# A four-layer graph network on one core: layer 3's rows for the first 20 node tiles stay in SBUF for layer 4

## The chip, the core and the metric

The kernel runs on one core of a Trainium2 chip. Its engines run in parallel, each through its own instructions in their order: PE (TensorE, matrix products into PSUM), ACT (ScalarE), DVE (VectorE), POOL (GpSimd, here the issuer of the gathers) and SP (SyncE, here an issuer of DMAs; ACT issues DMAs too). The metric is the device time of one execution in microseconds, the median of several runs. A profiled execution gives the lines that are quoted below.

## The reference

The input is x, 6250 nodes of 256 features, and 100,000 edges (src, dst) that are sorted by dst. Low-numbered nodes have by far the most edges. What is computed:

```python
h = relu(layernorm(x))
h = h @ W1_self + mean(h[src] by dst) @ W1_neigh + b1                    # layer 1
hp = relu(h @ W2_pool + b2_pool)
h = h @ W2_self + max(hp[src] by dst) @ W2_neigh + b2                    # layer 2, max-pooling
h = ((sum(h[src] by dst) + h) / (deg + 1)) @ W3_neigh + b3               # layer 3
h = h @ W4_self + mean(h[src] by dst) @ W4_neigh + b4                    # layer 4
out = x + h @ W_fc + b_fc
```

All of it is in fp32, with hidden width 512.

## The kernel before

The nodes are cut into 49 tiles of 128. The weight matrices that follow each other without a nonlinearity are multiplied with each other first, so that layers 3 and 4 have only sums over edges left to do on the nodes.

A sum over edges is done in one of two ways. For the first tiles, which have most edges (20 tiles in layer 3, `H3`; 22 in layer 4, `H4`), it is dense: a matrix A of edge counts, built before in fp8 and kept in DRAM as `tab_a`, is multiplied with the rows of all 49 source tiles (`dense`, the matmuls of L566 and L574 into `pd`). For the other tiles, POOL gathers the source rows, 128 edges at a time (L492), and PE adds them up with a one-hot matrix (L510 and L513 into `pg`); after every four gathers DVE adds the sum to `acc` (L542 and L544). `sums` writes both into one program: per gather one matmul of the gathered rows, and between them an even share of the dense matmuls, which a `Hub` hands out.

Layer 3 leaves, for each of the 49 tiles, 128 rows of two halves (`halves`: a rounded value and what the rounding left), 512 fp32 numbers, 256 KB a tile. `done3` writes them to DRAM as `tab_s`. For the 20 dense tiles it first adds `acc3`, 20 tiles of SBUF of the same size that hold the part of the sum that was made during the max-pooling layer.

Layer 4 (the block under `with tc.tile_pool(name="fl4"`) needs all 49 tiles of rows twice: the gathers read single rows from `tab_s`, and the dense matmuls need each tile whole in SBUF, as `Z4[s]`. Ten tiles (33 to 42) never leave SBUF: `done3` writes them into `zt33` and `zt38`. The other 39 are read back from `tab_s` by six loads on SP's queue (`resident`, L1817; `zt<-tab_s` in the profile). A is read in strips: `ac` is one strip, for one result tile and 5 to 7 source tiles, loaded through ACT's queue (L1785) nine strips ahead, and ACT widens it to `af` (L1794) four strips ahead. There are ten `ac` and six `af` buffers, so a strip can be widened when PE has finished the strip six before it.

The order of the source tiles is `order`: first the ten kept ones, then the loaded ones, for result tiles 0 to 3 together (their four sums lie in four PSUM banks), then tile after tile. The kept tiles' matmuls for result tiles 0 to 3, 40 of them, stand ahead of the first gathered matmul; the other 1038 are shared out over the gathers, four to five for each of the 266. The ring of gathered rows has 14 places: POOL's gather number n waits until PE has used number n-14.

When a result tile is complete, `done4` loads its rows of x and of `xq` (`xr` and `q`, through ACT's queue), DVE adds all up (L1910 and L1912), and SP stores it (L1915).

One rule of the built program matters here. Each DMA that SP or ACT issues takes one of eight semaphores in turn, in the program's order, and one that takes a semaphore waits until the semaphore's last user has landed. These semaphores are called counters below; rows of the order name them DMAHW0 to DMAHW7. So a load of a strip on ACT's queue can wait for a `zt` load on SP's, although it uses nothing of it, and whatever stands behind it on ACT waits too.

Of the kernel before, what the change touches and what calls it, by code (L numbers as in the profile page):

```python
# [9 lines left out]
F32 = mybir.dt.float32  # L10
# [3 lines left out]
F32R = mybir.dt.float32r  # L14
# [7 lines left out]
P = 128  # L22
# [15 lines left out]
def _edges_below(n, E, N):  # L38

    f = math.sqrt(min(n, N) / N)  # L40
    return E * f, Z_SIGMA * math.sqrt(E * f * (1.0 - f))
# [37 lines left out]
def fast_path(  # L79
# [18 lines left out]
    FH = W1_self.shape[1]  # L98
    FO = W_fc.shape[1]
    NT = (N + P - 1) // P  # L100
# [15 lines left out]
    for d in range(NT):  # L116
        m, s = _edges_below(d * P, E, N)
        m1, s1 = _edges_below((d + 1) * P, E, N)
# [9 lines left out]
    for d in range(NT):  # L128
        m, s = _edges_below(d * P, E, N)
        m1, s1 = _edges_below((d + 1) * P, E, N)  # L130
# [7 lines left out]
    H1, H3, H4 = HUB  # L138
# [524 lines left out]
    with ExitStack() as pro:  # L663
# [195 lines left out]
        nk = max(RB1, RB * P - RB1)  # L859
# [239 lines left out]
    with ExitStack() as on:  # L1099
# [35 lines left out]
        def done1(d, acc):  # L1135
# [37 lines left out]
            with behind(ended):  # L1173
                for k in range(KI):
# [11 lines left out]
                        lambda acc, d=d: todo.append(done1(d, acc)), extra=3)  # L1186
# [4 lines left out]
        hub = Hub(made.rest() + work)  # L1191
# [100 lines left out]
    span4 = ctx.enter_context(tc.tile_pool(name="span4", bufs=1))  # L1292
    upto3 = ctx.enter_context(ExitStack())
    span3 = upto3.enter_context(tc.tile_pool(name="span3", bufs=1))
# [2 lines left out]
    nc.scalar.dma_start(srcE, stash_e[0, :, jb - JC * P : T - JC * P].bitcast(I32))  # L1297
    keyE = span4.tile([P, T - jb], F32, name="keyE")
    nc.scalar.dma_start(keyE, stash_e[1, :, jb - JC * P : T - JC * P])
    acc3 = [span3.tile([P, FH], F32, name=f"acc3_{d}") for d in range(H3)]  # L1300
    begun = set()

    def add3(d, v):
# [12 lines left out]
    with tc.tile_pool(name="fl2c", bufs=1) as ck, ExitStack() as late:  # L1316
# [350 lines left out]
        hub = Hub(first, 12)  # L1667
# [12 lines left out]
        for b in reversed(range(NB)):  # L1680
# [3 lines left out]
            for s0 in range(0, tb, G2):  # L1684
                X = (xmore if at // G2 % 2 else xpool).tile([P, G2, FH], F32, name="X2")
                for k in range(G2):
# [27 lines left out]
                    if at == MADE_AT:  # L1714
                        for _ in steps:
# [3 lines left out]
                                                    name="kept_rows", bufs=1))  # L1719
# [101 lines left out]
    with ExitStack() as on:  # L1821
        psd = on.enter_context(tc.tile_pool(name="psd3", bufs=2, space=PSUM))
        psg = on.enter_context(tc.tile_pool(name="psg3", bufs=3, space=PSUM))
        psm = on.enter_context(tc.tile_pool(name="psm3", bufs=2, space=PSUM))
        one_tag[id(psm)] = "pm"
        zk = on.enter_context(tc.tile_pool(name="fz4", bufs=1, side="right"))
        Z4 = {}
        z4_kept = ((33, 38), (38, 43))
        z4_late = ((0, 7), (7, 14), (14, 20), (20, 27), (27, 33), (43, NT))
        for s0, s1 in z4_kept:  # L1830
            zt = zk.tile([P, s1 - s0, 2 * FO], F32R, name=f"zt{s0}", bufs=1)
            Z4.update({s: zt[:, s - s0, :] for s in range(s0, s1)})

        with tc.tile_pool(name="fl3", bufs=2) as wk:
            def done3(d, acc):
                q = wk.tile([P, FH], F32, name="q", bufs=2)
                if d < H3:
                    nc.vector.tensor_add(q, acc, acc3[d])
                    nc.vector.scalar_tensor_tensor(q, q, rgcn[:, d : d + 1], qrow,
                                                   op0=ALU.mult, op1=ALU.add)  # L1840
                else:
                    if d in Z3:
                        z = Z3[d]
                    else:
                        z = wk.tile([P, 3 * FH], BF16, name="zown", bufs=1)
                        with tc.issue_after(kept_stores[-1].ins):
                            nc.sync.dma_start(z, tab_r[d * P : (d + 1) * P, :])
                        yield 1
                        yield 1
                        yield 1  # L1850
                    if d < NT - 4:
                        for part in range(3):
                            nc.vector.tensor_add(acc, acc, z[:, part * FH : (part + 1) * FH])
                            yield 1
                    else:
                        own = bank(psm, "pm", "pm_own")
                        for part in range(3):
                            nc.tensor.matmul(own, ident_b, z[:, part * FH : (part + 1) * FH],
                                             start=(part == 0), stop=(part == 2))
                        yield 1  # L1860
                        nc.vector.tensor_add(acc, acc, own)
                    nc.vector.scalar_tensor_tensor(q, acc, rgcn[:, d : d + 1], qrow,
                                                   op0=ALU.mult, op1=ALU.add)
                q2 = Z4[d] if d in Z4 else wk.tile([P, 2 * FO], F32R, name="q2")
                halves(q[:, FO:], FO, q2)
                nc.sync.dma_start(tab_s[d * P : (d + 1) * P, :], q2.bitcast(F32))
                nc.sync.dma_start(xq[d * P : (d + 1) * P, :], q[:, :FO])
                yield 1

            late = ((0, 4), (4, KEPT), (EARLY[1], 45), (45, NT))  # L1870
            Z3 = {s: kept_rows[0][:, s, :] for s in range(KEPT)}
            with tc.issue_after(kept_stores[-1].ins):
                for s0, s1 in ((EARLY[1], NT),):
                    Z3.update(resident(wk, tab_r, FH, s0, s1))
            block = stream(wk, [(d, s0, s1) for d in range(H3) for s0, s1 in late], wk,
                           lambda s: s < KEPT)
            todo = []
            work = []
            for d in range(H3):
                work += dense([s for s0, s1 in late for s in range(s0, s1)], lambda s, d=d: block(d, s), lambda s: Z3[s], FH, psd,  # L1880
                              lambda acc, d=d: todo.append(done3(d, acc)), own=d,
                              halved=range(KEPT))
            sums(wk, psg, tab_r, FH, srcE, keyE, jb, H3, done3, 11, Hub(work), wait=14, todo=todo,
                 rest=12)

        upto3.close()
        settle(zk, on.enter_context(tc.tile_pool(name="flp", bufs=1, space=PSUM)))
        with tc.tile_pool(name="fl4", bufs=2) as wk:
            loaded4 = {}

            def load4(d):
                n = P if d < NFULL else NREM
                xr = wk.tile([P, FI], F32, name="xr4", bufs=10)
                nc.scalar.dma_start(xr[:n, :], x[d * P : d * P + n, :])
                q = wk.tile([P, FO], F32, name="q4", bufs=10)
                nc.scalar.dma_start(q[:n, :], xq[d * P : d * P + n, :])
                loaded4[d] = n, xr, q

            def done4(d, acc):
                for i in range(d, min(d + 3, H4 if d < H4 else NT)):  # L1900
                    if i not in loaded4:
                        load4(i)
                return finish4(d, acc)

            def finish4(d, acc):
                n, xr, q = loaded4.pop(d)
                yield 1
                yield 1
                yield 1
                nc.vector.tensor_add(xr[:n, :], xr[:n, :], q[:n, :])  # L1910
                for c in range(0, acc.shape[1], FO):
                    nc.vector.scalar_tensor_tensor(xr[:n, :], acc[:n, c : c + FO],  # L1912
                                                   rmean[:n, d : d + 1], xr[:n, :],
                                                   op0=ALU.mult, op1=ALU.add)
                nc.sync.dma_start(out[d * P : d * P + n, :], xr[:n, :])  # L1915

            order = [*z4_kept, *z4_late]
            first = range(4)
            block = stream(zk, [(d, *c) for c in order for d in first]
                           + [(d, *c) for d in range(4, H4) for c in order],  # L1920
                           wk, deep=9, ahead=4)
            todo = []
            parts4 = []
            for d in range(H4):
                parts4.append(dense([s for s0, s1 in order for s in range(s0, s1)],
                                    lambda s, d=d: block(d, s), lambda s: Z4[s], FO, (psd, psm)[d // 2 % 2],
                                    lambda acc, d=d: todo.append(done4(d, acc)), wide=True))
            nk = sum(s1 - s0 for s0, s1 in z4_kept)
            cuts = [sum(s1 - s0 for s0, s1 in order[:i]) for i in range(len(order) + 1)]
            hub = Hub([w for a, b in zip(cuts, cuts[1:]) for d in first for w in parts4[d][a:b]]  # L1930
                      + [w for p in parts4[4:] for w in p])
            hub.advance(4 * nk)
            for s0, s1 in z4_late:
                Z4.update(resident(wk, tab_s, FO, s0, s1))
            sums(wk, psg, tab_s, FO, srcE, keyE, jb, H4, done4, 14, hub, wait=4, todo=todo,
                 rest=8, wide=True)
# [643 lines left out]
```

## Time and profile before

| What | Value |
|---|---|
| runs before | 2724.58 us median of 3 (2719.38 to 2725.16) |
| the profiled execution's own time | 2732.06 us |
| its span | 2730.3 us |
| busy share of the span | PE 84%, DVE 76%, POOL 68%, ACT 48% |
| granted TensorE clock, mean | 0.924 of full |
| first gather of layer 4 | 2360.83 us from the start |
| last gather of layer 4 | 2712.28 us |
| bytes moved by DMA | 809.90 MB |

A row of a timeline reads: start in us, duration in us, engine, line of the kernel, operation, what it writes and reads, how many were merged into the row; in brackets, how long the engine had been idle and what ended that. A name such as SPq or ACTq is the engine's queue of DMAs. In a table of waits the engine and line stand on the left, what it waited for on the right, then the sum in us, the number of waits and the longest.

### The profile page before, as it was taken

The page shows a single profiled execution, that of the slowest core. Times are in us where ns is not written, and L with a number is a line of the kernel's source. Part 1 is how long each engine was busy: PE and PEld are TensorE (multiplying, and loading weights), DVE is VectorE, ACT ScalarE, POOL GpSimd, SP SyncE. Part 2 cuts the span into 40 slices and gives each one's busy share as a digit, 9 for nine tenths or more (in the row PEclk, how much of TensorE's full clock was granted, in tenths as well). Part 3 has the DMA queues.
Part 4 walks back from the last instruction along what each step waited for, and adds up shares of the span by engine and source line. Part 5 has one row for each costly group of instructions (what it writes and reads, how often), then busy time and mean ns, then how long its engine had stood idle before and what let it go on. Part 6 is the DMA issues. An engine that isn't in the chain of part 4 may idle for free.

```text
span 2730.3 us, 37722 instructions
## 1 busy us (share of the span) xinstructions
PE 2303.3 (84%) x10402; PEld 1436.1 (53%) x10402; DVE 2084.6 (76%) x5540; ACT 1301.6 (48%) x2859; POOL 1858.7 (68%) x2169
## 2 busy tenths in 40 slices
PE   4688999999787366566978999898799999879987
PEld 2356666777443132222645666655345445568766
DVE  8888777776489898888678998888467777557666
ACT  4467777764278888696422333232211111234443
POOL 5477777777567677677656676566477777667775
PEclk8799999999898578778989999999899999989999
DMA  8567777777699899899989999999799999999996
GB/s 272 157 178 206 209 206 212 217 222 232 200 356 341 295 343 346 290 322 358 342 288 305 339 343 318 283 321 311 283 380 385 378 383 363 333 364 351 315 302 216
DMA packets 365625, 809.90 MB, mean 297 GB/s; under 512 B 56238, under 2 KB 154646, under 8 KB 365372
## 3 DMA queue, kind: packets, MB, share of 16 engines
q0 software_dynamic: 143248, 501.86, 56.3%
q1 hardware_dynamic: 145928, 215.57, 21.7%
q10 hardware_dynamic: 76228, 89.96, 9.7%
q8 instruction: 85, 1.39, 0.2%
q14 instruction: 136, 1.11, 0.1%
HBM read 602.51 MB, written 205.46 MB: 296 GB/s over the span
## 4 chain that ended last, share of the span: by engine, by line
PE 49%; DMA 26%; DVE 13%; issue 5%; ACT 2%; POOL 2%; ACTq 0%; DVEq 0%; POOLq 0%; SPq 0%
PE pd L574 18%; PE pg L513 11%; DMA X<-rows,srcIf 9%; DMA ring<-tab_h,srcT 4%; DVE run L1669 3%; PE pm_hp L1175 3%; PE pm_prf L1558 3%; DMA rows<-X 2%; DMA xr<-in_x 2%; PE pm_hp L1169 2%; PE pb L349 2%; DVE acc L544 2%; DVE X L1669 2%; DMA out<-xr 2%; PE pm_prf L1552 2%
## 5 line engine op out<-in xcount | busy, mean ns | idle before, releaser
L1688 POOL DMA_INDIRECT X<-rows,srcIf x782 | 744.5, 952 | 368.0 <-issue 143.8
L1669 DVE SCALAR_TENSOR_TENSOR run<-run,samef,X 128x512 f32<-128x512 f32 x758 | 573.1, 756 | 52.8 <-DMA X<-rows,srcIf 47.1
L492 POOL DMA_INDIRECT ring<-tab_h,srcT x474 | 456.7, 963 | 150.1 <-issue 53.2
L513 PE MATMUL pg<-ring,hot 128*128 128x259 bf16 (+1 forms) x2292 | 475.1, 316 | 45.9 <-DMA ring<-tab_h,srcT 34.8
L544 DVE SCALAR_TENSOR_TENSOR acc<-pg,M,acc 128x256 f32<-128x256 f32 (+2 forms) x617 | 314.6, 536 | 79.5 <-PE pg L513 71.1
L492 POOL DMA_INDIRECT ring<-tab_r,srcE x290 | 292.1, 1007 | 117.1 <-issue 51.8
L1794 ACT CAST af<-ac 128x768 fp32r<-128x768 fp8e4 (+3 forms) x216 | 172.7, 805 | 384.7 <-DMA ac<-tab_a 193.4
L513 PEld LDWEIGHTS <-hot 128*128 128x128 bf16 x2292 | 214.0, 98 | 231.6 <-issue 108.7
L492 POOL DMA_INDIRECT ring<-tab_s,srcE x266 | 255.4, 960 | 110.5 <-PE pg L510 34.8
L566 PE MATMUL pd<-zt,af 128*128 128x512 f32 x1078 | 300.7, 402 | 33.5 <-ACT af L1794 30.5
L1669 DVE SCALAR_TENSOR_TENSOR X<-X,samef,run 128x512 f32<-128x512 f32 x379 | 282.3, 745 | 38.1 <-DMA X<-rows,srcIf 23.1
L574 PE MATMUL pd<-kept_rows,aw 128*128 128x512 f32 x920 | 293.9, 443 | 12.7 <-ACT aw L1624 6.5
L566 PEld LDWEIGHTS pd<-zt,af 128*128 128x128 f32 x1078 | 207.3, 194 | 86.2 <-ACT af L1794 38.9
L574 PEld LDWEIGHTS pd<-kept_rows,aw 128*128 128x128 f32 x920 | 175.8, 194 | 85.1 <-issue 35.3
L488 DVE TENSOR_SCALAR hot<-iota_bf,keyE 128x128 bf16<-128x128 bf16 (+1 forms) x556 | 143.9, 281 | 82.8 <-PE pg L513 51.9
L1558 PE MATMUL pm_prf<-unf,hTf 128*128 128x512 f32 x384 | 201.3, 649 | 1.9 <-ACT hTf L1548 1.3
L341 ACT ACTIVATE hs<-ht,onef 128x128 bf16<-128x128 bf16 x396 | 153.5, 393 | 90.6 <-PE pb L349 89.5
L1624 ACT CAST aw<-ae 128x512 fp32r<-128x512 fp8e4 x160 | 99.2, 621 | 188.0 <-PE pd L574 173.4
L574 PE MATMUL pd<-Z,A 128*128 128x256 bf16 (+1 forms) x1176 | 184.1, 273 | 0.8 <-ACT A L354 0.7
L375 ACT ACTIVATE ht<-iota_bf,skR 128x128 bf16<-128x128 bf16 x448 | 157.9, 402 | 12.8 <-DMA col<-in_L_gnn_b 8.9
L340 ACT ACTIVATE ht<-iota_bf,sk 128x128 bf16<-128x128 bf16 x396 | 153.1, 398 | 8.3
L393 PE MATMUL pb<-hm,hs 128*128 128x196 bf16 x448 | 82.2, 282 | 87.9 <-ACT A L398 77.5
(391 smaller groups left out, 4184.1 us busy)
## 6 DMA issues: line engine op xcount, KB each, us to landing
rows<-X SPq DMA_DIRECT2D x385, 256.0 KB, 4.8
tab_r<-r ACTq DMA_DIRECT2D x48, 384.0 KB, 4.7
rows<-hpf SPq DMA_DIRECT2D x49, 256.0 KB, 3.6
th<-tab_t ACTq DMA_DIRECT2D x49, 256.0 KB, 6.1
X<-rows,srcIf POOLq DMA_INDIRECT x782
tab_a<-A ACTq DMA_DIRECT2D x14, 784.0 KB, 6.6
ae<-tab_a SPq DMA_DIRECT2D x160, 64.0 KB, 4.9
tab_s<-q SPq DMA_DIRECT2D x39, 256.0 KB, 6.9
```

What stands on the lines that cost most here:

```text
L340: nc.scalar.activation(t, iota_b, AF.Abs, bias=sk[:, r : r + 1])
L341: nc.scalar.activation(hots[0], t, AF.Relu, bias=one, scale=-1.0)
L375: nc.scalar.activation(held["ht"][:, i, :], iota_b, AF.Abs, bias=sk[:, r : r + 1])
L492: nc.gpsimd.indirect_dma_start(out=ring[:, j % deep, :].bitcast(F32) if wide else ring[:, j % deep, :], out_offset=None, in_=table, in_off ...
L513: mm = nc.tensor.matmul(pg[:, : F + c], hot[j], X[:, part * F : (part + 1) * F + c], start=(k == 0 and part == 2), stop=(k == n - 1 and pa ...
L544: nc.vector.scalar_tensor_tensor(acc[d], half, m, acc[d], op0=ALU.mult, op1=ALU.add)
L566: nc.tensor.matmul(hold[0], a, z, start=(s == ss[0]), stop=(s == ss[-1]))
L574: nc.tensor.matmul(hold[0][:, : F + c], a, z[:, part * F : (part + 1) * F + c], start=(first and s != own), stop=(s == ss[-1] and part == ...
L1558: nc.tensor.matmul(pm, hT[:, c, :], un[:, c, :], start=False, stop=(c == KH - 1))
L1669: nc.vector.scalar_tensor_tensor(put, held, st, row, op0=ALU.mult, op1=ALU.max)
L1688: nc.gpsimd.indirect_dma_start(out=X[:, k, :], out_offset=None, in_=tab_p, in_offset=bass.IndirectOffsetOnAxis(ap=srcI[:, t : t + 1], axis=0),
L1794: nc.scalar.copy(wide[i][:, :n, :], got[i][:, :n, :])
```

## The change

`acc3` moves from a pool that ends with layer 3 to one that lasts to the kernel's end, at the same addresses. Each of its 20 tiles, once `done3` has added it, is given again under the same tag as `Z4[d]`, so layer 3's result rows of tiles 0 to 19 are written there and stay. They are still stored to `tab_s` for the gathers. Layer 4 no longer loads these 20 tiles, so three `zt` loads are left (19 tiles). The order of the source tiles becomes: tiles 0 to 19 first, then the ten kept ones, then the three loads. The number of matmuls that stand ahead of the first gathered one goes from 40 to 80 (`4 * H3`). Nothing is added to or taken from PE, DVE, ACT and POOL; SP has three DMAs fewer.

```diff
-    acc3 = [span3.tile([P, FH], F32, name=f"acc3_{d}") for d in range(H3)]
+    acc3 = [span4.tile([P, FH], F32, tag=f"acc3_{d}", name=f"acc3_{d}", bufs=1) for d in range(H3)]
...
+        z4_first = ((0, 7), (7, 14), (14, H3))
         z4_kept = ((33, 38), (38, 43))
-        z4_late = ((0, 7), (7, 14), (14, 20), (20, 27), (27, 33), (43, NT))
+        z4_late = ((H3, 27), (27, 33), (43, NT))
...
+                if d < H3:
+                    Z4[d] = span4.tile([P, 2 * FO], F32R, tag=f"acc3_{d}", name=f"z4_{d}", bufs=1)
                 q2 = Z4[d] if d in Z4 else wk.tile([P, 2 * FO], F32R, name="q2")
                 halves(q[:, FO:], FO, q2)
                 nc.sync.dma_start(tab_s[d * P : (d + 1) * P, :], q2.bitcast(F32))
...
-            order = [*z4_kept, *z4_late]
+            order = [*z4_first, *z4_kept, *z4_late]
...
-            nk = sum(s1 - s0 for s0, s1 in z4_kept)
             cuts = [sum(s1 - s0 for s0, s1 in order[:i]) for i in range(len(order) + 1)]
...
-            hub.advance(4 * nk)
+            hub.advance(4 * H3)
             for s0, s1 in z4_late:
                 Z4.update(resident(wk, tab_s, FO, s0, s1))
```

PE, from the last matmul of layer 3 on (`pm_own`); `zt_21030` and `zt_21031` are the kept tiles, `z_14` to `z_19` the change's new ones. Before:

```order
L1858 MATMUL pm_own<-zt_21035,ident_b 128x512
L566 MATMUL pd<-zt_21030,af 128x512 x20
L566 MATMUL pd<-zt_21031,af 128x512 x20
L510 MATMUL pg<-ring,hot 128x512 x5
L566 MATMUL pd<-zt_24800,af 128x512 x5
L510 MATMUL pg<-ring,hot 128x512
L566 MATMUL pd<-zt_24800,af 128x512 x4
```

With the change, the end of the 80 rows that now stand there:

```order
L566 MATMUL pd<-z_14_23708,af 128x512
L566 MATMUL pd<-z_15_23881,af 128x512
L566 MATMUL pd<-z_16_24090,af 128x512
L566 MATMUL pd<-z_17_24242,af 128x512
L566 MATMUL pd<-z_18_24443,af 128x512
L566 MATMUL pd<-z_19_24555,af 128x512
L510 MATMUL pg<-ring,hot 128x512 x5
L566 MATMUL pd<-zt_21030,af 128x512 x4
L510 MATMUL pg<-ring,hot 128x512
```

The first gathered matmul stands behind 80 dense ones, not 40, and the kept tiles come behind it.

ACT, a little behind that, where strips are loaded and widened. Of the change, with the counters:

```order
L1785 DMA ac_24796<-tab_a_69 128x320 [waits DMAHW6_49,Activation_49]
L1794 CAST af_24794<-ac_24739 128x768 [waits DMAHW7_49,PE_49]
L1785 DMA ac_24807<-tab_a_69 128x320 [waits Activation_49]
L1794 CAST af_24805<-ac_24751 128x768 [waits DMAHW1_49,PE_49]
L1785 DMA ac_24818<-tab_a_69 128x320 [waits DMAHW0_49,Activation_49]
L1785 DMA ac_24828<-tab_a_69 128x320 [waits Activation_49]
L1794 CAST af_24816<-ac_24763 128x640 [waits DMAHW2_49,PE_49]
```

Counted from 0, these are the loads of strips 15 to 18 and the widening of strips 10 to 12. The counters that strips 15 and 17 wait for (DMAHW6, DMAHW0) were last taken by the first and the second of the three `zt` loads; strip 22's load, five DMAs on, waits in the same way for the third. Before, the loads of strips 18, 22 and 29 wait in this way for the second, third and fifth of the six `zt` loads, and four of the six wait themselves: the third for the first, the fourth for strip 13, the fifth for the fourth, the sixth for strip 26.

DVE, in the first gathers of layer 4. Before, the first sum for a finished tile (L1910) stands behind four groups of four gathers:

```order
L544 SCALAR_TENSOR_TENSOR acc<-pg,M,acc 128x256 [waits DVE_49]
L542 TENSOR_SCALAR acc<-pg,M 128x256
L488 TENSOR_SCALAR hot<-iota_bf,keyE 128x128 [waits PE_49]
L544 SCALAR_TENSOR_TENSOR acc<-pg,M,acc 128x256 [waits DVE_49]
L1910 TENSOR_TENSOR xr_25125<-xr_25125,q_25127 128x256 [waits DMAHW6_49,DMAHW5_49]
```

With the change it stands behind the first group:

```order
L542 TENSOR_SCALAR acc<-pg,M 128x256 [waits PE_49]
L488 TENSOR_SCALAR hot<-iota_bf,keyE 128x128 [waits DVE_49]
L544 SCALAR_TENSOR_TENSOR acc<-pg,M,acc 128x256 [waits DVE_49]
L488 TENSOR_SCALAR hot<-iota_bf,keyE 128x128 [waits PE_49] x3
L1913 TENSOR_TENSOR xr_25179<-xr_25179,q_25181 128x256 [waits DMAHW4_49,DMAHW2_49]
L544 SCALAR_TENSOR_TENSOR acc<-pg,M,acc 128x256 [waits DVE_49,PE_49]
```

It waits for the loads of `xr` and `q` on ACT's queue; behind it stand the sums of the second group of gathers.

## Prediction

> **What bounds the kernel now.** The change touches layer 4 and the rows that layer 3 leaves, so I read the stretch from the start of layer 4 (2360 us) to the end: first the chain of work that ended last, then the waits of 2360 to 2430, then the timelines of POOL, PE and ACT. The chain, merged over 2355 to 2460:
>
> ```profile
> 2360.84 6.00 PE pd L566 x15
> 2366.88 8.24 DMA ac<-tab_a
> 2375.13 33.04 DMA zt<-tab_s
> 2408.19 8.46 DMA zt<-tab_s
> ```
>
> For 41 us (2375.13 to 2416.65) the chain lies on the loads that bring layer 3's rows back. The waits of 2360 to 2430 say who is held:
>
> ```profile
> DVE xr L1910 <- DMA q<-xq: 26.6, 3, 18.7
> PE pd L566 <- ACT af L1794: 20.7, 4, 8.8
> ACT af L1794 <- DMA zt<-tab_s: 19.2, 2, 10.9
> POOL ring L492 <- PE pg L510: 15.6, 7, 10.4
> PE pd L566 <- DMA zt<-tab_s: 3.0, 1, 3.0
> ```
>
> PE hardly waits for the rows themselves (3.0 us). It waits for widened strips, and ACT, which widens them and reads no row of `zt`, waits for `zt` loads: that is the shared counter. ACT's timeline shows two of the three places (strips 22 and 29):
>
> ```profile
> 2384.63 0.81 ACTq L1785 DMA_DIRECT2D ac<-tab_a  x2
> 2395.69 0.83 ACT L1794 CAST af<-ac 128x768 fp32r<-128x768 fp8e4 x1 [8.29 <-DMA zt<-tab_s]
> 2416.73 0.33 ACTq L1785 DMA_DIRECT2D ac<-tab_a  x1
> 2417.10 0.94 ACT L1794 CAST af<-ac 128x896 fp32r<-128x896 fp8e4 x1 [10.87 <-DMA zt<-tab_s]
> ```
>
> POOL is what the end hangs on. Undisturbed it starts a gather every 1.25 us:
>
> ```profile
> 2360.83 0.94 POOL L492 DMA_INDIRECT ring<-tab_s,srcE  x1 [13.47 <-DVE hot L488]
> 2378.34 0.95 POOL L492 DMA_INDIRECT ring<-tab_s,srcE  x1 [0.30 <-DMA ring<-tab_s,srcE]
> 2405.85 0.95 POOL L492 DMA_INDIRECT ring<-tab_s,srcE  x1 [0.30 <-issue]
> 2408.71 0.94 POOL L492 DMA_INDIRECT ring<-tab_s,srcE  x1 [1.91 <-PE pg L510]
> 2420.01 0.94 POOL L492 DMA_INDIRECT ring<-tab_s,srcE  x1 [10.36 <-PE pg L510]
> 2424.24 0.94 POOL L492 DMA_INDIRECT ring<-tab_s,srcE  x1 [1.16 <-PE pg L510]
> ```
>
> The row of 2424.24 is gather 40 (counted from 0; 2405.85 is gather 36). Undelayed it would start at 2360.83 + 40 x 1.25 = 2410.83, so POOL has lost 13.4 us there, all of it between 2407 and 2424, when the ring was full of rows that PE had not used. PE's side:
>
> ```profile
> 2360.84 11.80 PE L566 MATMUL pd<-zt,af 128*128 128x512 f32 x40 [5.63 <-ACT af L1794]
> 2372.48 1.33 PE L510 MATMUL pg<-ring,hot 128*128 128x512 f32 x5
> 2373.66 1.32 PE L566 MATMUL pd<-zt,af 128*128 128x512 f32 x5
> 2375.05 1.09 PE L566 MATMUL pd<-zt,af 128*128 128x512 f32 x4
> 2375.98 0.39 PE L510 MATMUL pg<-ring,hot 128*128 128x512 f32 x1
> 2384.69 0.47 PE L566 MATMUL pd<-zt,af 128*128 128x512 f32 x1 [2.96 <-DMA zt<-tab_s]
> 2396.57 1.22 PE L566 MATMUL pd<-zt,af 128*128 128x512 f32 x2 [3.68 <-ACT af L1794]
> 2400.05 1.09 PE L566 MATMUL pd<-zt,af 128*128 128x512 f32 x4
> 2418.09 1.22 PE L566 MATMUL pd<-zt,af 128*128 128x512 f32 x2 [8.80 <-ACT af L1794]
> ```
>
> A matmul takes (2375.98 - 2375.05) / 4 = 0.2325 us. With four to five dense ones and one gathered one per gather PE needs about 1.16 us against POOL's 1.25: once PE is behind by a full ring it makes good less than 0.1 us per gather, so a loss there stays.
>
> **The change part by part.**
>
> *Removed: 20 tiles of loads (5.2 MB) and their waits.* This removes the cause of the 13.4 us: -13.4 if nothing takes its place. The new tiles are ready long before, since layer 3 stores them one by one. In layer 3 the 20 tiles no longer wait for an earlier store of the same buffer; PE is busy there without a gap and covers that, so I take 0. The moved pool keeps its addresses: 0. The first widening still waits for the last store of layer 3, as the whole pool does: 0.
>
> *Moved: 40 more matmuls ahead of the first gathered one.* 40 x 0.2325 = 9.3 us, and 0.2 because the first strip is 896 wide (0.94 us, the row of 2417.10) and not 640 (0.73). The first gathered matmul goes from 2372.48 to 2382.0, its end to 2382.4. POOL's gather 14 reuses that ring place; its undisturbed start is the row of 2378.34. It now waits for PE until about 2382.7: +4.3, where before it waited for nothing. ACT can feed the 80: a 7-matmul strip takes PE 1.63 us and ACT 0.94 and an issue.
>
> *New: strips 15, 17 and 22 wait for the three remaining loads.* What SP's queue q1 moved in 2360 to 2372, in 2372 to 2384, and in 2412 to 2420 when POOL was held:
>
> ```profile
> q1 hardware_dynamic: 1034, 2.08, 52.7%
> q1 hardware_dynamic: 834, 1.68, 36.1%
> q1 hardware_dynamic: 1356, 2.72, 88.6%
> ```
>
> The first load (7 tiles, 1.84 MB) then lands near 2371, the second and third (1.57 MB each) at 1.68 / 12 = 0.14 MB/us near 2382 and 2393; POOL's pause lets them have up to 0.34 MB/us for a few us, so I take 2382 and 2390. Strip 15 waits till 2371, with strips 10 and 11 widened by 2375 and wanted at 2379: free. Strip 17 holds ACT till 2382; two issues (0.81) and a narrow strip later, at 2383.5, strip 12 is there, 0.3 late. Strip 22 holds ACT from 2386.5 to 2390, and behind it stands the widening of strip 15. PE's 15 matmuls of strips 12 to 14 and three gathered ones last till 2387.7; it goes on at 2390 + 0.8 + 0.73 = 2391.6. After such a wait its first eight matmuls took 2400.05 - 2396.57 = 3.5 us in place of 1.9. Counted through the ring, gather 24 is then 1.2 late: +1.2 (0 if the third load lands by 2387, +4 at 2393).
>
> The Trainium skill ("TensorE: Matmul & The Clock Gate", Part 1) puts the clock at half after an idle window of about 3.4 us; the 3.9 us here lie over that, and had they been 3 the 1.6 us of slow matmuls would fall away by the page. The rows show 3.68 us slow and 2.96 us not, so they do not contradict it.
>
> *Moved: DVE's first sum for a finished tile, now behind one group of gathers.* DVE waits there for `q`. Behind it stand the sums of group 1, whose PSUM bank gathered matmul 16 needs. Before, the wait cost DVE 18.7 us:
>
> ```profile
> 2400.81 0.33 ACTq L1896 DMA_DIRECT2D q<-xq  x1
> 2410.75 0.43 DVE L1910 TENSOR_TENSOR xr<-xr,q 128x256 f32<-128x256 f32 x1 [18.71 <-DMA q<-xq]
> q<-xq ACTq DMA_DIRECT2D x7, 128.0 KB, 4.9
> ```
>
> and hid under PE's own wait. Now ACT issues `q` about 5 us behind strip 22's load, at 2395; it lands at 2400 (4.9, the median) to 2405 (the 9.9 of the first). Matmul 16 is due near 2402.5. So 0 to +4; I take +1, near the median.
>
> *Later.* The start sums to -13.4 + 4.3 + 1.2 + 1 = -6.9. From there PE has 998 dense matmuls to share out and not 1038, 3.93 per gather for 4.09, which is 0.036 us a gather or 8 us over 230 gathers, and it starts on that 18 gathers earlier. Before, PE fell behind once more and was late at the end:
>
> ```profile
> 2674.26 0.95 POOL L492 DMA_INDIRECT ring<-tab_s,srcE  x1 [0.30 <-issue]
> 2677.08 0.94 POOL L492 DMA_INDIRECT ring<-tab_s,srcE  x1 [1.87 <-PE pg L510]
> 2679.21 0.94 POOL L492 DMA_INDIRECT ring<-tab_s,srcE  x1 [1.19 <-PE pg L510]
> 2712.28 0.95 POOL L492 DMA_INDIRECT ring<-tab_s,srcE  x1 [0.30 <-PE pd L566]
> 2717.58 1.97 PE L510 MATMUL pg<-ring,hot 128*128 128x512 f32 x8
> ```
>
> POOL's two starts after 2674.26 took 4.95 us in place of 2.50. With 8 us in hand this loss goes: -2.5 (0 if PE meets other waits). PE's last matmul ended 7.3 us after the last gather's start; a PE that keeps up needs only that gather's data: -1 (0 to -3).
>
> Sum: -6.9 - 2.5 - 1 = -10.4 us. The profiled execution took 2732.06, so 2721.7, or 0.38% less; the runs' median, 2724.58, is 7.5 lower, and on it the same 10.4 give 2714.2.
>
> **The rivals.** (1) *New waits eat most of it.* Strip 22's wait and `q` at their upper ends (+4 and +4) and no later gain: -13.4 + 4.3 + 8 = -1.1; halfway from there to the forecast's start, -4: 2720.6. For it: both waits lie where the ring is full, so each us counts. Against it: each upper end needs a transfer far slower than its nearest rows.
>
> (2) *Slower: the three loads land together.* Now they stand in SP's queue with nothing between; if they share the bandwidth, the first lands near 2391 with the last. Strip 15 then holds ACT from 2370, strips 10 and 11 are missing, and PE stops at matmul 69 (2379). It goes on at 2393 with twelve matmuls at half rate (5 us), gather 14 starts at 2398.5, 20.2 late in place of 13.4: +6.8, 2731. It decides when the first load lands after 2384, where the loss equals today's. Against it: the first `zt` load's rows were in use at 2373.66 while the second came at 2384.6 (rows of 2384.63 and 2384.69), so they went one after the other. The Trainium skill ("DMA: Bandwidth & Descriptors", Queues, rings and completion order) says that descriptors are consumed in ring order, which agrees, but also that completion is not FIFO per issuing engine, which is this rival's opening.
>
> (3) *The 80 matmuls are not fed.* If strips 9 to 11 land late (a strip took up to 8.2 us, the chain's second row), each us of PE's wait before the first gathered matmul is one of POOL's: at 5 us of wait the gain is 5.4 (2719.2), at 10 it is gone (2724.2), beyond that the kernel is slower.
>
> **How the numbers follow.** Forecast 0.58, rival (1) 0.22, (2) 0.08, (3) 0.12. A measurement tells a change from none at about 0.2%, 5.4 us, so the border is 2719.1. The forecast lies under it, rival (1) for two fifths: faster 0.67. Slower comes from (2) and a third of (3): 0.12. The rest, 0.21, is the same. The forecast's own range is 2705 (13.4 + 2.5 + 3 - 4.3 = 14.6 less, and 5 for the spread of the runs, 2719.38 to 2725.16) to 2719; to leave out no more than 2 in 10 it goes on over (1) to 2725.
>
> **What would show it.** Right: POOL's gather 14 near 2382.7 and gather 40 near 2417.3 if layer 4 starts at 2360.8; three `zt` loads landing near 2371, 2382 and 2390; one PE wait of 3 to 5 us, ended by ACT, near 2390; no ring stall late in the layer; 5.2 MB fewer moved. Wrong: gather 14 later than 2385 (the 80 not fed, or loads together), a DVE wait on `q` with POOL held behind it after 2400, or POOL on time and an end that PE sets anyway.

## The result, and the profile after

The changed kernel takes 2716.11 us (median of 20 runs, 2705.9 to 2729.43), the kernel before 2726.75 us on the same chips (20 runs, 2718.38 to 2742.98). The ratio is 0.9955, with a 95% interval of 0.9943 to 0.9966: 12.3 us less, 9.3 to 15.5 (the two medians lie 10.6 apart). The profiled execution of the changed kernel took 2714.39 us, its span is 2712.6.

The profiled spans differ by 17.7 us. Of these, 4.1 lie ahead of layer 4, whose first gather starts at 2356.69 instead of 2360.83. I don't count them as an effect of the change: in the other profiled executions of this study on such chips that start lies anywhere between 2347.6 and 2362.3. What the change did is read from the start of layer 4, which lasts from its first gather to the end of the span: 369.4 us before, 355.9 after, 13.5 less. A second profiled execution of the changed kernel (`after_again`, below) gave 355.8. "Late" means here, as in the prediction, how far a gather starts behind the first one's start plus 1.25 us for each gather between.

| Layer 4 | before | after |
|---|---|---|
| first gather | 2360.83 | 2356.69 |
| gather 14 late by | 0.0 | 3.9 |
| gather 40 late by | 13.4 | 4.2 |
| gather 265, the last, late by | 20.2 | 7.2 |
| last gather to the end | 18.0 | 17.5 |

The chain of work that ended last, after, merged over 2351 to 2456:

```profile
2356.31 22.01 DMA zt<-tab_s
2380.08 1.20 PE pd L566 x4
2381.52 0.92 PE pd L566 x4
```

The loads hold the chain for 22 us, not 41, and behind them it is PE's own matmuls. The waits of 2356 to 2426, after:

```profile
DVE xr L1913 <- DMA q<-xq: 10.7, 4, 8.2
PE pd L566 <- ACT af L1794: 7.2, 2, 5.8
POOL ring L492 <- PE pg L510: 6.0, 7, 4.2
```

No wait of ACT is put down to a `zt` load in this table (19.2 us before; one of 9.44 us that belongs there is named below), and POOL waits for PE 6.0 us in place of 15.6. The timelines of POOL, PE, ACT and DVE, after:

```profile
2356.69 0.94 POOL L492 DMA_INDIRECT ring<-tab_s,srcE  x1 [13.46 <-DVE hot L488]
2378.10 0.94 POOL L492 DMA_INDIRECT ring<-tab_s,srcE  x1 [4.21 <-PE pg L510]
2695.14 0.95 POOL L492 DMA_INDIRECT ring<-tab_s,srcE  x1 [0.30 <-DVE hot L488]
...
2356.92 20.68 PE L566 MATMUL pd<-z,af 128*128 128x512 f32 x80 [5.84 <-ACT af L1794]
2377.44 1.29 PE L510 MATMUL pg<-ring,hot 128*128 128x512 f32 x5
2380.08 1.20 PE L566 MATMUL pd<-zt,af 128*128 128x512 f32 x4 [1.35 <-ACT af L1794]
...
2379.31 0.72 ACT L1794 CAST af<-ac 128x640 fp32r<-128x640 fp8e4 x1 [9.44 <-PE pg L510]
2382.58 0.81 ACTq L1785 DMA_DIRECT2D ac<-tab_a  x2
...
2391.15 0.43 DVE L1913 TENSOR_TENSOR xr<-xr,q 128x256 f32<-128x256 f32 x1 [8.15 <-DMA q<-xq]
```

The 80 matmuls run without a gap and end at 2377.6. The row of 2378.10 is gather 14, which waited 4.21 us for PE. Strip 12 is missing for 1.35 us at 2380: ACT widened it after 9.44 us, in which it stood on the load of strip 17 and so on the second `zt` load (the row names PE; in the second execution the same wait, 10.0 us, is put down to `zt`). The row of 2382.58 begins with strip 22's load, so the third `zt` load had landed by 25.9 us into the layer, and PE was not stopped by it. DVE waits 8.15 us for `q`, and nobody waits for DVE there.

What the prediction did not look at is how full the DMA engines are. These rows give, for stretches of layer 4, the granted clock, the DMA share (the time of all packets as a share of the 16 engines' time; it can come out a little above 1) and GB/s in the last three columns, first before, then after:

```profile
2361.00:2400.00 39.00, 32.36 (x122) 25.35 (x123) 10.01 (x33) 14.28 (x18) 29.55 (x32) 0.90 1.02 388
2400.00:2480.00 80.00, 68.57 (x283) 55.28 (x283) 50.09 (x157) 32.53 (x39) 50.59 (x53) 0.89 1.02 359
2560.00:2640.00 80.00, 71.43 (x300) 54.78 (x298) 47.83 (x150) 33.88 (x40) 60.66 (x63) 1.00 0.94 309
```

```profile
2361.00:2400.00 39.00, 37.65 (x164) 30.59 (x163) 10.19 (x36) 18.44 (x25) 26.56 (x29) 0.99 1.05 392
2400.00:2480.00 80.00, 78.45 (x337) 62.12 (x336) 62.91 (x193) 36.39 (x44) 60.80 (x64) 1.00 1.02 357
2560.00:2640.00 80.00, 70.99 (x300) 55.09 (x299) 49.83 (x156) 32.56 (x39) 60.80 (x64) 1.00 0.93 304
```

The DMA engines are full in the first 120 us of layer 4, and over 90% busy 200 to 280 us into it, in both kernels, while POOL's own share of the last stretch is 61 of 80 us. The change takes 5.25 MB off SP's queue (215.57 to 210.32 MB in the page's part on queues), and nothing from the others. What that leaves room for shows in the first 70 us of the layer: both kernels move 372 to 373 GB/s there, but before, 10.33 MB of it went over SP's queue and 11.08 MB to the gathers, and after, 5.66 and 13.11 MB.

### The profile page after: what moved, and what is told of

Its sections match the earlier page's. It is cut to its first block, busy times and chain, and to the rows that moved or that the text cites. A ratio compares the mean times of both kernels' runs of the same rounds, so it can differ in the third digit from the quotient of the medians.

```text
span 2712.6 us, 37694 instructions
## 1 busy us (share of the span) xinstructions
PE 2304.6 (85%) x10402; PEld 1432.5 (53%) x10402; DVE 2085.8 (77%) x5540; ACT 1298.6 (48%) x2859; POOL 1856.7 (68%) x2169
## 3 DMA queue, kind: packets, MB, share of 16 engines
q1 hardware_dynamic: 143320, 210.32, 21.4%
## 4 chain that ended last, share of the span: by engine, by line
PE 50%; DMA 24%; DVE 13%; issue 4%; ACT 3%; POOL 2%; ACTq 0%; SPq 0%; DVEq 0%; POOLq 0%
PE pd L574 18%; PE pg L513 11%; DMA X<-rows,srcIf 8%; DVE run L1669 4%; DMA rows<-X 3%; DMA ring<-tab_h,srcT 3%; PE pd L566 3%; PE pm_hp L1175 3%; PE pm_prf L1558 3%; DMA xr<-in_x 3%; PE pm_hp L1169 2%; DVE X L1669 2%; PE pb L349 2%; DMA out<-xr 2%; PE pm_prf L1552 2%
## 5 line engine op out<-in xcount | busy, mean ns | idle before, releaser
L513 PE MATMUL pg<-ring,hot 128*128 128x259 bf16 (+1 forms) x2292 | 475.3, 316 | 39.9 <-DMA ring<-tab_h,srcT 29.4
L1794 ACT CAST af<-ac 128x896 fp32r<-128x896 fp8e4 (+3 forms) x216 | 171.9, 805 | 379.6 <-DMA ac<-tab_a 168.9
L566 PE MATMUL pd<-zt,af 128*128 128x512 f32 x638 | 177.6, 395 | 5.7 <-ACT af L1794 5.7
L488 DVE TENSOR_SCALAR hot<-iota_bf,keyT 128x128 bf16<-128x128 bf16 x474 | 125.7, 274 | 39.0 <-PE pg L513 37.9
```

What stands on the lines that cost most here:

```text
L488: nc.vector.tensor_scalar(hot[j], iota_b, keyT[:, j - jb : j - jb + 1], None, op0=ALU.is_equal)
L513: mm = nc.tensor.matmul(pg[:, : F + c], hot[j], X[:, part * F : (part + 1) * F + c], start=(k == 0 and part == 2), stop=(k == n - 1 and pa ...
L566: nc.tensor.matmul(hold[0], a, z, start=(s == ss[0]), stop=(s == ss[-1]))
L1794: nc.scalar.copy(wide[i][:, :n, :], got[i][:, :n, :])
```

## The experiments

Three theories stood against each other. *Counters*: before, ACT was held by `zt` loads through the shared counters, and that cost the 13.4 us (the prediction). *Rows*: the loaded rows came too late for PE, with or without the counters. *Bytes*: the DMA engines are full, and each MB costs time whoever waits for it.

The runs stood against the kernel before on the same chip each time:

| Run | us, median | ratio to before, 95% | layer 4, us | gather 40 late | last late |
|---|---|---|---|---|---|
| before_spaced | 2729.29 | 1.0007, 0.9993 to 1.0020 | 370.5 | 8.4 | 21.1 |
| unused | 2732.52 | 1.0022, 1.0009 to 1.0034 | 375.2 | 12.0 | 27.3 |
| unused_spaced | 2739.44 | 1.0043, 1.0026 to 1.0059 | 377.3 | 12.5 | 29.5 |
| front60 | 2718.11 | 0.9962, 0.9947 to 0.9977 | 360.5 | 3.9 | 11.4 |
| after_again | 2712.08 | 0.9949, 0.9932 to 0.9966 | 355.8 | 3.3 | 7.5 |
| spaced60_again | 2708.83 | 0.9946, 0.9932 to 0.9960 | 354.0 | 1.7 | 5.3 |
| ring19_spaced_again | 2713.18 | 0.9960, 0.9946 to 0.9974 | 363.6 | 0.3 | 8.7 |
| unused_late | 2728.14 | 1.0009, 0.9993 to 1.0026 | 372.0 | 4.7 | 24.0 |

The first four shared one group of runs of before (median 2726.47), the last four another (2724.08).

### before_spaced: the same loads, placed apart

In the kernel before, each `zt` load is put in the program's order behind the load of one strip (`stream` calls `placed` with each strip's load; `behind` fixes the order alone and waits for nothing):

```diff
+            place = dict(zip((10, 17, 23, 28, 32, 36), z4_late))
+            def placed(i, ins):
+                if i in place:
+                    Z4.update(resident(wk, tab_s, FO, *place[i], behind=ins))
...
-            for s0, s1 in z4_late:
-                Z4.update(resident(wk, tab_s, FO, s0, s1))
```

> The kernel before with the same six zt loads, but their places in the program are spread: each is put behind the load of strip 10, 17, 23, 28, 32 and 36, so that its counter comes round to ACT's queue only when it should have landed. Bytes, order and PE's work are unchanged. Theory 'counters' (the prediction's): ACT no longer waits for zt loads, PE waits a few us for rows at most; gather 40 starts 0 to 5 us behind its undisturbed time instead of 13.4, and the run is 8 to 13 us shorter, near 2716. Rival 'rows': the loads land no earlier than before, since they share the DMA engines with the gathers (0.14 MB/us, while 28 dense matmuls use 1.84 MB in some 8 us), and PE waits for zt itself: gathers 40 to 60 are 10 to 16 us late, and the time is within 4 us of the kernel before.

The time is that of the kernel before, 1.0007. The waits of PE for rows and strips, and of ACT for `zt`, in the first 70 us of its layer 4:

```profile
PE pd L566 <- DMA zt<-tab_s: 14.1, 3, 8.1
PE pd L566 <- ACT af L1796: 5.6, 1, 5.6
ACT af L1796 <- DMA zt<-tab_s: 11.3, 1, 11.3
```

```profile
2377.94 0.76 PE L566 MATMUL pd<-zt,af 128*128 128x512 f32 x1 [5.73 <-DMA zt<-tab_s]
2404.47 1.19 PE L566 MATMUL pd<-zt,af 128*128 128x512 f32 x2 [8.07 <-DMA zt<-tab_s]
```

PE now waits for no strip but the very first, and 14.1 us for the rows themselves (3.0 before). The loss has changed its name and not its size.

The run does not do what it was made for, though. ACT was still held by counters of `zt` loads, in this table for 11.3 us (19.2 before), ahead of a load of `xr`. That cost PE nothing of its own: the load of `xr` went out at 2404.35, when the `zt` load had landed that PE waited for in the row of 2404.47. And SP's loads were held in their turn: in its queue's table of waits (2345 to 2440) the `zt` loads waited 29.4 us for one another, 19.1 for loads of `q` and 8.2 for a strip. Between some of them the queue stood nearly still. In 2360 to 2364 SP's queue (the first row) moved 0.04 MB while the gathers' queue (the second) moved 1.12:

```profile
q1 hardware_dynamic: 23, 0.04, 2.4%
q0 software_dynamic: 347, 1.12, 69.1%
```

So the run shows that the time stays when PE's waits for strips go, and not that the counters cost nothing: how much of the 14.1 us these pauses make, and how much the counters cost in the kernel before, stays open. None of the arrangements tried here was without held counters. What speaks for the bytes is that holding a queue left the DMA engines no emptier. In the first 70 us of the layer their share was 1.01 before (372 GB/s), 1.02 here (378) and 1.03 in the changed kernel (373).

### unused and unused_spaced: the bytes back, for nobody

Both start from the changed kernel. For `unused`, behind the three `zt` loads:

```diff
+            for s0 in range(0, H3, 5):
+                spare = wk.tile([P, 5, 2 * FO], F32, name="spare", bufs=1)
+                nc.sync.dma_start(spare, tab_s[s0 * P : (s0 + 5) * P, :].rearrange("(c p) f -> p c f", p=P))
```

> The changed kernel, and behind its three zt loads SP reads the 20 tiles back after all (four loads of 1.31 MB into one spare buffer that nobody reads). Nobody needs the rows; bytes and counters are back. Theory 'counters': strips wait for three of the four spare loads, ACT is held, PE stops, and 4 to 10 us are lost against the changed kernel (2720 to 2726). Theory 'rows' (PE's need for the rows cost the time): 0 to 2 us. Theory 'bytes' (the traffic itself slows gathers and strips): 4 to 10 us, and the same in the next run.

> As the run before, but each spare load is put in the program behind the load of strip 23, 27, 31 and 35, so that no strip's load or widening comes upon its counter while it is in flight (the next users are loads of xr, 8 DMAs on). Theories 'counters' and 'rows': 0 to 2 us against the changed kernel (2716 to 2718). Theory 'bytes': 4 to 10 us, as much as with the spare loads close together.

`unused` gives back all that the change had gained and more: 0.67% of 2726 us, 18 us, and the theory of rows alone (0 to 2 us) is out. `unused_spaced` loses another 6 us (0.21%). But it was no fair test of counters against bytes: the next users of the spare loads' counters, loads of `xr`, stand on ACT's queue too and held it. The waits of `unused_spaced` in the first 70 us of the layer:

```profile
PE pd L566 <- ACT af L1796: 15.6, 5, 5.8
ACT af L1796 <- issue: 8.7, 2, 8.3
ACT af L1796 <- DMA spare<-tab_s: 5.9, 1, 5.9
```

In `unused` ACT is held by spare loads as well (5.2 us). So these two show that reading the tiles back costs the gain even when no matmul needs them, and not by which way.

### unused_late: the same bytes from 80 us on

As `unused_spaced`, with other strips:

```diff
+            place = dict(zip((60, 75, 90, 105), range(0, H3, 5)))
```

> The changed kernel with the four spare loads (5.2 MB) of the run unused, but behind the loads of strips 60, 75, 90 and 105, that is from about 100 us into layer 4 on, when the three zt loads are long done and the DMA engines move 300 to 340 GB/s in place of 400. Each of the four still leaves its counter to a later load of a strip. If the bytes cost only where the DMA engines are full, 0 to 2 us against the changed kernel (16 us in unused). If 5.2 MB cost the same anywhere, or a large load costs through its counter anywhere, 4 us or more.

It takes 0.60% more than the changed kernel on the same chip (1.0009 against 0.9949), 16 us, and layer 4 is 16.2 us longer. The four loads are issued at 2442.92 to 2548.70 in a layer that starts at 2362.3, so from 81 us on. The expectation was wrong in its premise: at that point the DMA engines have no room (a share of 0.98 in the changed kernel from 80 to 200 us in). The counters are nearly out of the way here: ACT is held by the first spare load alone, from 2448.6 to 2457.4, in which PE did not wait for ACT, and by none of the other three. (The table of waits puts this one, 9.2 us, down to PE; the trace has the semaphore ahead of the strip's load of 2457.47 released by the spare load.) PE waits where the profile of the changed kernel has smaller waits or none, in 2450 to the end:

```profile
POOL ring L492 <- PE pg L510: 34.2, 64, 4.5
PE pg L510 <- issue: 14.9, 6, 4.0
PE pd L566 <- ACT af L1796: 13.0, 11, 2.5
```

and in the same part of the changed kernel, 2450 to its end:

```profile
POOL ring L492 <- PE pg L510: 11.9, 39, 0.3
PE pd L566 <- ACT af L1794: 6.7, 7, 1.7
PE pg L510 <- issue: 6.3, 3, 3.6
```

POOL waits three times as long for PE, and PE twice as long both ahead of gathered matmuls and for strips. What PE waited for ahead of the gathered ones the profile doesn't name ("issue"). The timelines of PE and DVE show it, here for the longest of these waits:

```profile
2524.17 0.47 PE L510 MATMUL pg<-ring,hot 128*128 128x512 f32 x1 [4.04 <-issue]
2520.50 0.42 DVE L1918 TENSOR_TENSOR xr<-xr,q 128x256 f32<-128x256 f32 x1 [5.58 <-DMA xr<-in_x]
2523.59 0.48 DVE L544 SCALAR_TENSOR_TENSOR acc<-pg,M,acc 128x256 f32<-128x256 f32 x1
```

DVE stood 5.58 us on a load of `xr`, and behind it the sums that free `pg` for the next group of four gathers. PE starts 0.1 us after the last of them ends (2524.07). It is the same for the wait of 3.87 us at 2696.65 (DVE had waited 7.07 us for `xr`). This is the way that the prediction feared for `q`, only late in the layer. It was not the gathered rows: that gather had started 15.6 us before (2508.52), and where PE did wait for rows in this run, 1.50 us at 2451.81, they were there 8.2 us after their gather's start.

The total price is shown, 16 us for 5.24 MB here and 18 at the start. That it is the bytes divided by the rate is not. By that estimate, at the 309 to 359 GB/s of the rows of 2400 to 2640, they occupy the DMA engines for 15 to 17 us, which fits. But the lateness did not all come while they moved. At gather 152, just after the last of them had landed, the run was 13.8 us late against 5.6 in the changed kernel, so 8.2 us of the price were there. The other 8.7 came up to the last gather, most of it at gather 250, which found the ring full when PE stopped at 2696.65, and there the DMA share is lower (0.83 from 2567 to the end).

Such a stop, of 2.4 to 3.9 us, 316 to 342 us into the layer, is in all ten profiles from chips like the first. The changed kernel has it too:

```profile
2673.12 0.76 PE L510 MATMUL pg<-ring,hot 128*128 128x512 f32 x1 [3.60 <-issue]
2670.63 0.42 DVE L1913 TENSOR_TENSOR xr<-xr,q 106x256 f32<-106x256 f32 x1 [6.68 <-DMA xr<-in_x]
```

There PE was far enough ahead for POOL not to notice. A version that comes to this stop with its ring nearly full pays for it.

### front60: gather 14's wait taken away

```diff
-            hub.advance(4 * H3)
+            hub.advance(3 * H3)
```

> The changed kernel with 60 dense matmuls ahead of the first gathered one instead of 80; the other 1018 are shared out, 4.01 per gather. The prediction's term of +4.3 for gather 14: 60 x 0.2325 = 14 us, PE frees the first ring place before POOL wants it at 17.5, so gather 14 starts on time and gather 40 is 0.3 late instead of 4.2: 3 to 4 us gained, 2712. Rival: without POOL's pause of 4 us the zt loads get less of the DMA engines, the third lands 3 to 4 us later than the 26 us it took, the load of strip 22 holds ACT and PE stops 2 to 4 us near 30 us into the layer: gain under 2 us, 2714 to 2716.

The rival came true. Gather 14 starts on time, and gather 40 is 3.95 us late in place of 4.21. POOL's pause came back as PE's wait for a strip, which ended 33 us into the layer (the timelines of PE and of ACT):

```profile
2393.51 1.65 PE L566 MATMUL pd<-zt,af 128*128 128x512 f32 x3 [6.36 <-ACT af L1794]
2384.08 8.12 ACTq L1785 DMA_DIRECT2D ac<-tab_a  x3
```

The second row is ACT's issue of the loads of strips 21 to 23. It took 8.12 us: strip 22's stood on its counter until the third `zt` load had landed, 30.8 us into the layer. In the changed kernel POOL's pause lets that load through: in 2376 to 2383, SP's queue (the first row) moved 0.23 MB/us (1.60 MB in 7 us) against the 0.14 that it had in 2372 to 2384 before:

```profile
q1 hardware_dynamic: 803, 1.60, 58.7%
q0 software_dynamic: 276, 0.91, 31.9%
```

From number 40 to the last the gathers lose 7.5 us, against 3.0 in the changed kernel. Of this, 4.0 us came at gathers 250 to 253, at the stop named above (3.45 us of PE here). The 4.01 dense matmuls per gather in place of 3.93 do not explain it: `spaced60_again`, below, has the same 4.01 and loses 3.6.

### spaced60, ring19, ring19_spaced and ring19_spaced60: first on a slower chip

The edits, on the changed kernel: for `spaced` the three `zt` loads are placed as in `before_spaced`, behind the loads of strips 10, 16 and 21; 60 stands for `3 * H3` as above; for `ring19`:

```diff
-            sums(wk, psg, tab_s, FO, srcE, keyE, jb, H4, done4, 14, hub, wait=4, todo=todo,
+            sums(wk, psg, tab_s, FO, srcE, keyE, jb, H4, done4, 19, hub, wait=4, todo=todo,
```

> 60 dense matmuls ahead, as in front60, and the three zt loads placed in the program behind the loads of strips 10, 16 and 21, so that ACT comes upon their counters (strips 16 and 23, then a load of q) only when they should have landed. Theory 'counters hold ACT': with 39 tiles gone no dense matmul needs a loaded row before 30 us, so the 6.4 us that PE waited for a strip at 2393 in front60 came from strip 22's counter alone; here it goes, gather 40 is under 1 us late (3.95 in front60), and the time is 3 to 4 us under the changed kernel, near 2712.5. Rival 'bytes': the DMA engines are full, the strips themselves come late, PE waits 3 us or more for ACT anyway, and gather 40 is again 3 to 4 us late.

> The changed kernel with 19 places in the ring instead of 14 (10 KB a partition, out of what the loads had used). POOL may run 6.25 us further ahead: gather 14 does not wait (4.3 us late before). Without that pause strip 22's load holds ACT as in front60, and PE, 4 us behind already, stops some 6 us: together about 10 against a margin that is 6.25 larger, so gather 40 is 1 to 2 us late, the last 3 us less late than in the changed kernel: 2713. Rival: what PE loses at the start has to be made good at under 0.1 us per gather, the deeper ring only moves the wait to later gathers, and gather 60 is 4 us late or more: no gain.

> Both: 19 places, the three loads placed behind strips 10, 16 and 21, and 80 dense matmuls ahead. If both mechanisms stand, neither gather 14 nor any up to 60 waits for PE, the only growth left is the slow one (3 us from gather 40 to the last in the changed kernel): the last gather 3 us late instead of 7.2, the time 4 us under the changed kernel, 2712. If the bytes set it, gather 40 is 3 us late or more.

> As the run before with 60 dense matmuls ahead, 4.01 shared out per gather instead of 3.93. If PE's share decides how late the layer ends (front60 lost 7.5 us from gather 40 to the last, the changed kernel 3.0), the last gather is 2 to 4 us later than with 80; if the deeper ring covers the late waits, the two agree within 1 us.

These four came to a chip on which the kernel before took 3112.22 us (35 runs). There the ratios are 0.9988 (0.9958 to 1.0019), 0.9995 (0.9973 to 1.0017), 0.9987 (0.9958 to 1.0016) and 0.9967 (0.9941 to 0.9992). From gather 40 on they came 1.47 us apart in `spaced60`, and the last was 56 us late in each, whatever the start did, so the expectations are not answered by these runs. Two of the kernels were run again on a chip like the first, with the changed kernel beside them.

### after_again, spaced60_again and ring19_spaced_again

> The changed kernel unchanged, as the control for the three runs beside it on the same chip. On a chip like the first: 0.995 of the kernel before, gather 40 of layer 4 4.2 us late and the last 7 us; on a chip like that of the last four runs, where every gather came slower, the ratio is near 0.999 and the last gather is some 56 us late whatever the start does.

> The same kernel as spaced60, since a chip on which every gather is late says nothing on the start. 'Counters hold ACT': no wait of PE for a strip after the first, gather 40 under 1 us late, 3 to 4 us under the changed kernel on this chip. 'Bytes': a wait of PE of 3 us or more for ACT between 20 and 40 us into the layer, gather 40 3 to 4 us late.

> The same kernel as ring19_spaced. If gather 14's wait in the changed kernel is a real cost, it and all its consequences go here: gather 40 under 1 us late, the last 3 us, 4 us under the changed kernel on this chip. If the bytes of the first 40 us set it, gather 40 is 3 us late or more.

`after_again` repeats the changed kernel: ratio 0.9949, layer 4 within 0.1 us. `spaced60_again` comes out between its theories: gather 40 is 1.7 us late, and PE waits twice for a strip, 1.54 and 3.67 us. The second wait is a counter's again, for ACT stood on a load of `q` until the third `zt` load had landed:

```profile
2387.94 0.73 ACT L1796 CAST af<-ac 128x640 fp32r<-128x640 fp8e4 x1 [4.83 <-DMA zt<-tab_s]
```

Its layer 4 is 1.8 us shorter than that of `after_again`, its median 3.3 us lower, and the two ratios (0.9946 and 0.9949) can't be told apart. Against `front60`, which differs from it in the placing alone, gather 40 is 2.2 us less late. So strip 22's counter cost something, but less than the 4.3 that was to be had.

`ring19_spaced_again` does at the start what it was made for, gather 40 is 0.3 us late, and gains nothing: its median is 1.1 us above that of `after_again`. The timelines of POOL and PE near the end show why:

```profile
2673.69 0.95 POOL L492 DMA_INDIRECT ring<-tab_s,srcE  x1 [3.30 <-PE pg L510]
2672.95 0.47 PE L510 MATMUL pg<-ring,hot 128*128 128x512 f32 x1 [3.37 <-issue]
```

PE is behind by the whole deeper ring, stops for 3.37 us (the stop named above, behind a wait of 5.90 us of DVE for `xr`), and from there works off four dense and one gathered matmul after the other to the end. Its last gather starts 23.7 us ahead of the end (17.0 in `after_again`). POOL running ahead is worth nothing when PE is what comes after it. No version here beats the changed kernel by more than can be measured.

## Why the prediction was right in its number, and what became of its cause

- **The number.** 2714.2 was forecast, 2716.11 measured; 10.4 us less was forecast, 12.3 (9.3 to 15.5) measured, 13.5 in the profiled layer 4. None of the three rivals came: the 80 matmuls were fed (20.68 us in one row), the loads did not land together, the new waits did not eat the gain.
- **-13.4, the waits of the `zt` loads.** The size held: gather 40 is 9.2 us less late, which is 13.4 less the 4.2 that came new. The step that the runs don't bear out is its cause, "that is the shared counter". When PE no longer waited for strips it waited for the rows, and the time was the same (`before_spaced`, where counters held SP's loads, so that the counters' own share stays open). And the same bytes cost 16 us where nobody needed them and only one of their four loads held ACT (`unused_late`). The prediction read who waited for whom. It took the queue's rate, 0.14 MB/us, as given, and did not ask why it was so low: its own row gave SP's queue 36.1% of the DMA engines, and the stretch of 2361 to 2400 has them full.
- **+4.3 for gather 14.** Measured 3.9, and 3.2 in `after_again`. Right as a row, too high as a price: without it gather 40 is as late in `front60`, and 1.6 us less late in `spaced60_again` than in `after_again`.
- **+1.2 for strip 22.** Measured 0. The loads were to land 10, 21 and 29 us into the layer. The second did, at 21.7. The third was there at 25.9, and at 30.8 in `front60`, where POOL did not pause: the pause left it more of the DMA engines than I took. PE stopped for strip 12 alone, 1.35 us for the 0.3 forecast, with no cost to POOL: gather 24 is as late as gather 15.
- **+1 for `q`.** Measured 0. DVE waited 8.15 us, with PE never behind it. The mechanism is real, but it stops PE later, through `xr`: 3.60 us at 2673.12, which cost POOL nothing.
- **-2.5 later.** Measured -3.8: from gather 40 to the last the lateness grows by 3.0 us in place of 6.8. Before, a stop of PE made POOL lose 2.5 us (gathers 238 and 239). A stop like it, 3.60 us, is there after as well, but no longer fills the ring, and so far the prediction was right. That fewer dense matmuls per gather bring this about is not shown: `front60` and `spaced60_again`, both at 4.01, grow by 7.5 and 3.6 us, and `after_again`, at 3.93, by 4.2.
- **-1 at the end.** Measured -0.5 (18.0 to 17.5 us from the last gather).

The terms are off by -1.3 to +0.5 us, and together the profiled layer 4 gained 3.1 us more than forecast. That the sum was near does not make the account right. It priced waits one by one, around a resource that was full; `front60` and `before_spaced` show that such a wait, taken away in one place, can come back in another.

## What to carry to other kernels

Before charging a wait to its releaser, look at the DMA share of that stretch. Where it is near 1, ask what a change takes off the queues, and don't expect much of a rearrangement: 5.2 MB more cost 16 us or more here in three arrangements, 5.25 MB fewer gained 12.3, and none of the re-placings of the same bytes gained anything that could be measured. Bytes divided by the rate (some 15 us) came near the total, but part of the price fell due later, at a stop that a kernel with some lead passes unnoticed. A wait that the chain shows through a shared semaphore can be the place where a late transfer is noticed first, and not its cause; the test is to take the semaphore out and see whether the time goes, and to check in the trace that it is out. Where the profile says "issue", look at what the other engines finished just then. A deeper buffer ahead of an engine helps only if that engine catches up before the end.

## What the runs showed of the hardware

The chips differ. On the slower one, a stretch of 140 us from 40 us into layer 4 of the `spaced60` kernel held 97 gathers and 294 GB/s at a DMA share of 0.91; on the other, the same kernel and stretch held 111 gathers and 341 GB/s at 0.99 (in each row, the last count in brackets is POOL's):

```profile
2744.00:2884.00 140.00, 124.33 (x484) 94.94 (x483) 85.81 (x262) 52.20 (x63) 91.34 (x97) 0.94 0.91 294
```

```profile
2392.00:2532.00 140.00, 138.98 (x602) 111.88 (x601) 100.45 (x314) 64.01 (x77) 106.06 (x111) 1.00 0.99 341
```

The gathers' queue in these two stretches, the slower chip first:

```profile
q0 software_dynamic: 7655, 25.11, 54.7%
```

```profile
q0 software_dynamic: 8758, 28.72, 56.9%
```

Its packets took a tenth more time per byte on the slower chip (54.7 / 25.11 against 56.9 / 28.72). Why is open; a ratio from one chip need not hold on another.

TensorE's clock fell after a shorter wait than the one in the prediction's rows (3.68 us). In `after_again`, a wait of 2.26 us was followed by matmuls at half rate, and the granted clock (third column from the end) fell with them:

```profile
2378.01 1.70 PE L566 MATMUL pd<-zt,af 128*128 128x512 f32 x4 [2.26 <-ACT af L1794]
2379.93 1.91 PE L566 MATMUL pd<-zt,af 128*128 128x512 f32 x4
2380.00:2382.00 2.00, 2.00 (x7) 1.57 (x6) 0.29 (x1) 0.00 (x0) 1.58 (x2) 0.53 1.09 403
```

Four matmuls took 1.91 us, then 1.09 again from 2381.98 on. In the kernel before, a wait of 2.96 us was followed by none of this: the granted clock from 2384.6 to 2388 is 1.00. So the length of the wait alone does not decide. The Trainium skill ("TensorE: Matmul & The Clock Gate", Part 1) says that the clock falls after an idle window of about 3.4 us and that these windows run freely and don't start anew with the kernel. A free-running window agrees with a longer wait that did no harm; a whole idle window does not fit into 2.26 us, and there the measurement decides.
